# Graph layer pair on one core: the third hop in seven products, with the result transposed back in 128-row blocks

## The chip, the cores and the metric

The kernel runs on one core of one Trainium2 chip. The metric is the time of one execution on the device, in microseconds (us). Lower is better.

## The reference, cut to what matters

The input is `x`, 8 batches of 2048 nodes with 64 features, and `adj`, a 2048 x 2048 matrix. Each row of `adj` has about ten entries that are not zero, and all of one row are equal: `adj[n, m] = r[n]` where two nodes are joined or equal, else 0. Two layers follow each other, each ends in a layer norm over the 64 features.

```python
# layer 0: K = 3, weights of their own for each node, from an embedding of 16 numbers
w = einsum('nd,dkio->nkio', embedding, weight)
As = [I, A, 2*(A @ A) - I]
out = einsum('bnki,nkio->bno', einsum('knm,bmc->bnkc', stack(As), x), w) + einsum('nd,do->no', embedding, bias)
x = layernorm(x + out)
# layer 1: both supports are adj
x_stack = [x0, A x0, 2 A (A x0) - x0, A x0, 2 A (A x0) - x0]
out = concatenate(x_stack, -1) @ weight + bias          # (5*64, 64)
x = layernorm(x + out)
```

So each layer needs `A` and `A A` applied to something. In layer 1 the features can be multiplied by the weights first, and that is what the kernel does: with `u2`, `u1`, `u0` = the normed features times three 64 x 64 matrices, the output is `u0 + A (u1 + A u2)`.

## The kernel before, in words

`kernel()` calls `gnn_kernel`, which runs `pattern` (the fast path, all that is timed here) and, if a flag says that `adj` has not the form told above, `general`.

The matrix is used as a mask of zeros and ones (`s`, exact in the float32r type), and the row's value `r` is multiplied in afterwards. A feature tile (128 nodes by 512 numbers, 8 batches x 64) is split in a high and a low half (`high` on ScalarE, L209; `low` on VectorE, L213), so that each product is two float32r matmuls. There are 16 tiles of 128 nodes. `z[0]`, `z[1]`, `z[2]` hold three such sets of tiles in SBUF.

There are four hops, with layer 0's mixing between the second and the third.

1. *First hop* (`hop_x`, `add_block` L229): `A x`, 512 matmuls, in two halves of eight output tiles. Masks are made by `places` (L198: not equal 0). Alongside, `put_together` writes sums and differences of the four quarters of the mask (L393) to device memory as bfloat16, `sums_of`, from GpSimd's queue, and `seen` (L445) counts the entries.
2. *Second hop* (`seven_products`): `A (A x)` by seven products of quarter matrices rather than eight. A product is eight steps; a step has 8 matmuls (L529) with the feature sum as the stationary operand, and the mask sum (256 KB from `sums_of`, cast by ScalarE at L517) or the mask itself (a 512 KB slab and `places`) as the moving one. The result is therefore transposed, features by nodes, which is what layer 0's mixing needs. `put` adds each product into the quarters of `z[2]` that need it (L550). 448 matmuls.
3. *Layer 0's mixing* (`mix0`, one tile of 128 nodes after another): for each of two halves of the batches and four groups of embedding numbers, 12 matmuls on float32 (L342, two instructions each), and four accumulations on VectorE that weight the result by the embedding (L348). Before the last group, `between()` transposes the normed features of the tile before (`transpose`, L268, copied by ScalarE at L270) and `A x` of the next tile. After the tile, `layernorm` (L306 to L312) and `project` of the tile before (L361, L368, L369) give `u2`, `u1`, `u0` in `z[0]`, `z[1]`, `z[2]`.
4. *Third hop* (`hop_h`): `A u2` for output tiles 0 to 3, 8 to 15 and 4 to 7, each group over 16 steps; a step makes its mask with `places_equal` (L205: equal to the row's value, with a count) and the halves of `z[0][k]`. 512 matmuls (L229). `evict` (L260 on VectorE; L257 and L258 on ScalarE and GpSimd) adds `r` times the sum to `z[1]`.
5. *Fourth hop*: output tiles 0 to 7 by `hop_g`, 16 steps of 16 matmuls, which also keeps the halves of `z[1]` for later; then tiles 8 to 15 one at a time by `hop_tile`, each in two halves of 16 matmuls. Behind it run the last norms (`square_sums`, `rsqrt`) and the stores.

What sets the order: `run(steps)` goes through a list of steps, and every step has parts with a lead (a part with lead 2 is written two steps ahead of the use). After each step two entries of the list `todo` are written. While `in_order` is not empty, `ordered(...)` keeps instructions in the order of the program on their engine; otherwise the tile framework's scheduler may move them. Loads go on SyncE's queue in program order. PSUM is a pool of four tiles of two banks each, handed on in turn (`bank`).

The last tile of layer 0 is projected inside the third hop: `hop_h`'s last step of the first group does it, and only there does `in_order` begin.

Of the kernel before, what the change touches and what calls it, by code (L numbers as in the profile page):

```python
# [8 lines left out]
F32 = mybir.dt.float32  # L9
# [28 lines left out]
def pattern(  # L38
# [20 lines left out]

    nc = tc.nc  # L60
# [13 lines left out]
    rowpool = pool(hops, "frow", 1, side="right")  # L74
    hpool = pool(hops, "fhl", HL, side="right")
# [23 lines left out]
    equal = keep.tile([P, 3 * NT], F32, tag="equal", name="equal")  # L99
# [13 lines left out]
    v = const.tile([P, 3, C], F32, tag="v", name="v")  # L113
# [122 lines left out]
    def run(steps):  # L236

        got = [{} for _ in steps]
        for i in range(-6, len(steps)):
            for ahead in range(6, -1, -1):  # L240
                for lead, part in steps[i + ahead] if 0 <= i + ahead < len(steps) else ():
                    if lead == ahead:
                        part(got[i + ahead])
            for _ in range(2):
                if todo and i >= 0:
                    todo.pop(0)()
# [15 lines left out]
    def transpose(src, tag, pt=None):  # L262
# [7 lines left out]
        nc.scalar.copy(  # L270
            tt.rearrange("p j (h n) -> p h j n", h=2), pt[:, :, : B // 2 * C].rearrange("p h (j n) -> p h j n", n=C)
        )
# [5 lines left out]
    def rsqrt(ss):  # L278
# [6 lines left out]
        nc.vector.scalar_tensor_tensor(va, ss, 1.0 / C, eps.to_broadcast(list(ss.shape)), ALU.mult, ALU.add)  # L285
        sd = col("ln_sd")
        nc.scalar.activation(sd, ss, AF.Sqrt, bias=eps, scale=1.0 / C)  # L287
        r0 = col("ln_r0")
        nc.vector.reciprocal(r0, sd)

        q = col("ln_q")
        nc.vector.scalar_tensor_tensor(q, r0, -0.5, r0, ALU.mult, ALU.mult)
        nc.vector.tensor_tensor(q, q, va, ALU.mult)
        r = col("ln_r")
        nc.vector.scalar_tensor_tensor(r, q, 1.5, r0, ALU.add, ALU.mult)
        return r

    def square_sums(src, to):
        sq = work.tile([P, B, C], F32, tag="ln_sq", name="sq")
        nc.scalar.activation(sq, src, AF.Square)  # L300
        nc.vector.tensor_reduce(to, sq, AX.X, ALU.add)

    def layernorm(src):

        s = work.tile([P, B], F32, tag="ln_s", name="s")
        nc.vector.tensor_reduce(s, src, AX.X, ALU.add)  # L306
        nc.vector.tensor_tensor(s, s, part, ALU.mult)  # L307
        xc = xcpool.tile([P, B, C], F32, tag="ln_xc", name="xc")
        nc.gpsimd.tensor_tensor(xc, src, wide(s), ALU.subtract)  # L309
        ss = work.tile([P, B], F32, tag="ln_ss", name="ss")  # L310
        square_sums(xc, ss)
        nc.gpsimd.tensor_tensor(xc, xc, wide(rsqrt(ss)), ALU.mult)  # L312
        return xc
# [7 lines left out]
    def mix0(t, tt, between):  # L321
# [4 lines left out]
        for g in range(2):  # L326
# [6 lines left out]
            for dg in range(D // DG):  # L333
                if g == 1 and dg == D // DG - 1:
                    between()
# [10 lines left out]
                for d in range(DG):  # L346
                    dd = dg * DG + d
                    nc.vector.scalar_tensor_tensor(  # L348
                        part, pm[:, :, :, d, :].rearrange("p j i c -> p (j i) c"), emb_sb[:, t, dd : dd + 1], part, ALU.mult, ALU.add
                    )  # L350
        return layernorm(acc)

    def project(t, hT, pus=None):


        for g in range(2):
# [9 lines left out]
            bs = slice(4 * g, 4 * g + 4)  # L366
            for s in range(2):
                nc.scalar.copy(bc(s, t)[:, bs, :].rearrange("p (i j) c -> p j i c", j=2), got[:, :, :, 2 - s, :])  # L368
            nc.vector.tensor_tensor(  # L369
                bc(2, t)[:, bs, :].rearrange("p (i j) c -> p j i c", j=2), got[:, :, :, 0, :],  # L370
                bias1.unsqueeze(1).unsqueeze(1).to_broadcast([P, 2, 2, C]), ALU.add,
            )
# [10 lines left out]
    S1, S2, S4, S3 = range(4)  # L383
    couple = []
# [11 lines left out]
    def hop_x(g, kk, j):  # L396
# [37 lines left out]
        def use(got):  # L434
# [8 lines left out]
            seen = work.tile([P, 2, Q], BF16, tag="ln_sq", name="seen")  # L443
            i = g * NT + k
            ordered(nc.scalar.activation(seen, s, AF.Copy, accum_out=nonzero[:, i : i + 1]))  # L445
            if last and g == 1:

                todo.extend(lambda i=i: out(i) for i in range(4, 8))
# [11 lines left out]
    def seven_products(s, to, more):  # L460
# [3 lines left out]
        sums, kept = [], {}  # L464

        def sum_of_y(kk, name):
# [11 lines left out]
            if name == "T2":  # L478
# [4 lines left out]
                return add(y, add(y, quarter(2, 2), quarter(1, 2), ALU.subtract), quarter(1, 1), ALU.add)  # L483
            y = xcpool.tile([P, BC], F32, tag="ln_xc", name="y")
            if name == "T4":
                return add(y, kept[kk // 2][:, kk % 2], quarter(2, 1), ALU.subtract)
# [3 lines left out]
        def step(p, kk):  # L490
# [5 lines left out]
            def y_high(got):  # L496
                hl = hpool.tile([P, 2, BC], F32R, tag="hl", name="hl")
                got["hl"] = [hl[:, 0], hl[:, 1]]
                if name[0] == "B":
                    sum_y(got)  # L500
# [5 lines left out]
            def load_sum(got):  # L506
                if isinstance(which, tuple):
                    return
                raw = got["raw"] = rawp.tile([P, 2, Q], BF16, tag="raw", name="raw")
                load(nc.sync, raw, sums_of[kk, :, :, which, :].rearrange("g m n -> m g n"))  # L510

            def operands(got):
                if isinstance(which, tuple):
                    got["s"] = places(slab(kk + KK * which[1], which[0] * HALF, HALF))
# [7 lines left out]
            def use(got):  # L522
# [10 lines left out]
                if p == 0 and kk == 3:  # L533
                    node_bias(sums[1])
                    todo.extend(lambda h=h: keep_node_bias(sums[1], h) for h in range(2))
                if kk < KK - 1:
                    return
                if p < 6:
                    todo.extend([lambda: None] * 4)
                for i in range(2):  # L540
                    for c in range(2):
                        todo.append(lambda i=i, c=c: put(acc[i][:, c], i, c))
                todo.extend(more.get(p, ()))
# [21 lines left out]
            before = [(5, sum_y)] if name[0] != "B" else []  # L565
# [8 lines left out]
    def times_r(t):  # L574
# [6 lines left out]
    pieces = weights()  # L581
    more = {
        1: [lambda: ordered(next(pieces)) for _ in range(13)],
        5: [lambda: times_r(0), lambda: times_r(1)],
    }
    run([hop_x(g, kk, j) for g in range(2) for kk in range(KK) for j in range(2)] + seven_products(1, to_z2, more))
# [13 lines left out]
    def hop_h(g, first, n, k):  # L600
        def operands(got):
            if g == 0 and k == NT - 1:
                project(mixed[0], transpose(mixed[1].rearrange("p b c -> p (b c)"), "hT"))
                layer0.close()
                in_order.append(True)
            i = g * NT + k
            raw = slab(k, first * P, n * P)
            got["s"], got["hl"] = places_equal(raw, first * P, equal[:, i : i + 1]), halves(z[0][k])

        def use(got):  # L610
            s, hl = got["s"], got["hl"]
            if k == 0:
                accs[:] = banks(n)
            add_block(accs, s, hl, k == 0, k == NT - 1)
            if k == NT - 1:
                for i, a in enumerate(accs):
                    evict(z[1][first + i], first + i, a, i % 2)

        return [(2, operands), (0, use)]

    third = [hop_h(g, first, n, k) for g, (first, n) in enumerate(((0, 4), (8, 8), (4, 4))) for k in range(NT)]

    mixed = None
    tt = operands(0)
    for t in range(NT):
        done = {}

        def between():
            if mixed is not None:
                done["hT"] = transpose(mixed[1].rearrange("p b c -> p (b c)"), "hT")  # L630
# [5 lines left out]
        new = t, mix0(t, tt, between)  # L636
        tt = done.get("tt")
        if mixed is not None:
            project(mixed[0], done["hT"])
        mixed = new  # L640
# [7 lines left out]
    def check():  # L648
# [3 lines left out]
        tc.keep_in_program_order(nc.vector.tensor_tensor(bad, count("n_nz", nonzero), count("n_eq", equal), ALU.not_equal))  # L652
        tc.keep_in_program_order(nc.vector.tensor_add(bad, bad, count("n_0", zeros)))
        ones = work.tile([P, 1], F32, tag="ones", name="ones")
        tc.keep_in_program_order(nc.vector.memset(ones, 1.0))
        pf = bank("pf")
# [11 lines left out]
    EARLY = 8  # L668
    late = []
    ks = [0, 1, 2, 3, 8, 9, 10, 11, 12, 13, 14, 15, 4, 5, 6, 7]  # L670
    hls = {}
    sums = keep.tile([P, 8, B], F32, tag="sums", name="sums")
    late_values = {}

# [384 lines left out]
```

## Time and profile before

| | us |
|---|---|
| median of 3 runs (837.89 to 840.62) | 839.54 |
| the profiled execution's own time | 839.63 |
| its span, first to last instruction | 837.6 |
| mean granted TensorE clock | 0.994 |
| first hop, first to last matmul step | 5.9 to 122.5 |
| second hop | 122.5 to 225.3 |
| layer 0's mixing, up to the third hop's first matmul | 225.3 to 592.0 |
| third hop and the fourth's steps | 592.0 to 769.9 |
| the fourth hop's tiles | 769.9 to 827.8 |
| last norm and store | 827.8 to 837.6 |

The span is what the profiler recorded between the first and the last instruction; the time of the execution has 2.0 us more around it. All engines share one time axis. PE is TensorE's matmuls, PEld its weight loads, DVE VectorE, ACT ScalarE, POOL GpSimd, SP SyncE. In a group of instructions the columns are: line, engine, operation, output <- inputs, sizes, count, then busy time and mean nanoseconds of one, then the engine's idle time before them and what ended it. Matmuls overlap each other, so a mean duration of 390 ns goes with a step of less than 230 ns from start to start. A line can be that of a helper.

### The profile page before, as it was taken

The numbers are of one execution on the slowest core, as the hardware profiler recorded it, in microseconds if no ns is written. First come the engines' busy times: TensorE is split into PE (matmuls) and PEld (weight loads), VectorE is DVE, ScalarE is ACT, GpSimd is POOL, SyncE is SP. The second block draws the span as 40 slices with busy tenths as digits, with TensorE's granted clock in tenths as the row PEclk, the third lists the DMA queues.
The fourth block names the chain that finished last, engine by engine and source line by source line (L and its number), as shares of the span: only waits on it lengthen the run. The fifth ranks groups of instructions, "written<-read, shape, count | busy, mean of one in ns | idle before, by whom it ended". The sixth has DMA issues, their size and how long they took to land.

```text
span 837.6 us, 14392 instructions
## 1 busy us (share of the span) xinstructions
PE 823.5 (98%) x5614; PEld 732.0 (87%) x5614; DVE 607.0 (72%) x1256; ACT 224.6 (27%) x427; POOL 128.8 (15%) x130
## 2 busy tenths in 40 slices
PE   9999999999999999999999999989999999999995
PEld 6888888888888999999999999989888878888884
DVE  6868657757878888888788888897867567534662
ACT  5436445772002111111111111101331132401210
POOL 0100000002731111111111111020101020102133
PEclk9999999999999999999999999999999999999998
DMA  9976775558200000000000000120256227544462
GB/s 332 394 273 221 248 258 174 154 163 289 88 14 14 11 6 13 14 14 13 14 14 13 14 14 14 42 86 2 76 182 190 94 74 240 173 142 126 132 183 92
DMA packets 57180, 96.55 MB, mean 115 GB/s; under 512 B 3984, under 2 KB 28816, under 8 KB 56976
## 3 DMA queue, kind: packets, MB, share of 16 engines
q1 hardware_dynamic: 52208, 82.69, 30.6%
q0 software_dynamic: 2304, 8.39, 3.0%
q10 hardware_dynamic: 2592, 4.47, 1.5%
q8 instruction: 47, 0.77, 0.4%
q14 instruction: 29, 0.24, 0.1%
HBM read 82.94 MB, written 12.58 MB: 114 GB/s over the span
## 4 chain that ended last, share of the span: by engine, by line
PE 93%; DVE 4%; issue 1%; DMA 0%; ACT 0%; POOL 0%; SPq 0%; DVEq 0%; POOLq 0%
PE pm L342 36%; PE acc L229 35%; PE accT L529 12%; PE a L229 7%; DVE acc L348 3%; PE pu L361 2%; PE pt L268 1%; PE first L133 1%; DVE s L205 0%; DMA raw<-in_adj 0%; POOL got L318 0%; DVE s L306 0%; ACT L287 0%; PE accT L144 0%; POOL xc L309 0%
## 5 line engine op out<-in xcount | busy, mean ns | idle before, releaser
L229 PE MATMUL acc<-hl,s 128*128 128x512 f32 x1280 | 292.7, 390 | 0.3 <-DVE acc L348 0.3
L229 PEld LDWEIGHTS acc<-hl,s 128*128 128x128 f32 x1280 | 239.4, 188 | 52.9 <-issue 1.2
L348 DVE SCALAR_TENSOR_TENSOR acc<-pm,pack_sb,acc 128x256 f32<-128x256 f32 x512 | 246.3, 483 | 43.5 <-PE pm L342 21.1
L342 PE MATMUL pm<-w,xt 64*128 64x256 f32 x1024 | 161.1, 379 | 3.1 <-DVE acc L348 2.8
L342 PE MATMUL pm<-w,z 64*128 64x256 f32 x1024 | 160.4, 378 | 0.0
L342 PE MATMUL pm<-w,t 64*128 64x256 f32 x1024 | 160.1, 377 | 0.2 <-ACT t L270 0.2
L342 PEld LDWEIGHTS pm<-w,xt 64*128 64x128 f32 x1024 | 108.1, 188 | 5.6 <-issue 1.8
L342 PEld LDWEIGHTS pm<-w,t 64*128 64x128 f32 x1024 | 110.7, 188 | 2.0 <-ACT t L270 0.6
L342 PEld LDWEIGHTS pm<-w,z 64*128 64x128 f32 x1024 | 110.8, 188 | 1.4
L198 DVE TENSOR_SCALAR s<-raw 128x1024 fp32r<-128x1024 f32 x87 | 68.1, 783 | 57.8 <-PE acc L229 48.8
L529 PE MATMUL accT<-s,hl 128*128 128x512 f32 x448 | 102.0, 389 | 0.0
L529 PEld LDWEIGHTS accT<-s,hl 128*128 128x128 f32 x448 | 84.0, 188 | 17.5
L209 ACT CAST hl<-z 128x512 fp32r<-128x512 f32 (+1 forms) x120 | 67.0, 578 | 119.1 <-PE acc L229 108.5
L213 DVE TENSOR_TENSOR hl<-z,hl 128x512 fp32r<-128x512 f32 (+1 forms) x120 | 81.5, 681 | 13.6 <-ACT hl L209 10.7
L205 DVE SCALAR_TENSOR_TENSOR s<-raw,rrow 128x512 fp32r<-128x512 f32 (+1 forms) x48 | 45.8, 956 | 26.7 <-PE acc L229 25.3
L270 ACT COPY hT<-pt 128x512 f32<-128x512 f32 x16 | 9.4, 586 | 204.4 <-PE pt L268 204.4
L309 POOL TENSOR_TENSOR xc<-acc,s 128x512 f32<-128x512 f32 x16 | 17.1, 1068 | 282.4 <-DVE s L307 282.4
L229 PE MATMUL a<-hl,s 128*128 128x512 f32 x256 | 58.5, 390 | 0.0
L229 PEld LDWEIGHTS a<-hl,s 128*128 128x128 f32 x256 | 48.0, 188 | 10.0
L258 POOL TENSOR_TENSOR z<-z,got 128x512 f32<-128x512 f32 x12 | 18.8, 1592 | 155.2 <-ACT got L257 155.1
L328 POOL TENSOR_TENSOR acc<-z,ebias 128x256 f32<-128x256 f32 x32 | 27.0, 866 | 87.1 <-ACT hl L209 85.6
L517 ACT CAST s<-raw 128x1024 fp32r<-128x1024 bf16 x32 | 33.6, 1050 | 10.6 <-ACT hl L209 10.6
(87 smaller groups left out, 477.0 us busy)
## 6 DMA issues: line engine op xcount, KB each, us to landing
raw<-in_adj SPq DMA_DIRECT2D x103, 512.0 KB, 4.5
raw<-in_adj SPq DMA_DIRECT2D x34, 256.0 KB, 3.0
sums_of<-z POOLq DMA_DIRECT2D x16, 512.0 KB, 4.9
raw<-sums_of SPq DMA_DIRECT2D x32, 256.0 KB, 2.8
xt<-in_xT SPq DMA_DIRECT2D x16, 256.0 KB, 2.7
out<-got ACTq DMA_DIRECT2D x16, 256.0 KB, 2.0
z<-in_x SPq DMA_DIRECT2D x15, 256.0 KB, 9.3
w<-in_w SPq DMA_DIRECT2D x3, 512.0 KB, 5.8
```

Of the source, the lines that this page charges most:

```text
L198: ordered(nc.vector.tensor_scalar(s, raw, 0.0, None, ALU.not_equal))
L205: ordered(nc.vector.scalar_tensor_tensor(s, raw, 0.0, r, ALU.add, ALU.is_equal, accum_out=count))
L209: ordered(nc.scalar.copy(to[0], src))
L213: ordered(nc.vector.tensor_tensor(to[1], src, to[0], ALU.subtract))
L229: nc.tensor.matmul(accs[i], lhsT=s[:, i * P : (i + 1) * P], rhs=hl[h], start=(first and h == 0), stop=(last and h == 1),)
L258: ordered(nc.gpsimd.tensor_tensor(to, to, got, ALU.add))
L309: nc.gpsimd.tensor_tensor(xc, src, wide(s), ALU.subtract)
L328: nc.gpsimd.tensor_tensor(part.rearrange("p (j i) c -> p j i c", j=2), bc(0, t)[:, 4 * g : 4 * g + 4, :].rearrange("p (i j) c -> p j i c", ...
L342: nc.tensor.matmul(pm[:, j, i], lhsT=tt[k][q, 2 * g + i, :], rhs=w[k][q, ds, :], start=(k == 0), stop=(k == 2),)
L348: nc.vector.scalar_tensor_tensor(part, pm[:, :, :, d, :].rearrange("p j i c -> p (j i) c"), emb_sb[:, t, dd : dd + 1], part, ALU.mult, ALU.add
L517: ordered(nc.scalar.copy(s, got["raw"]))
L529: nc.tensor.matmul(acc[i][:, c], lhsT=hl[h][:, i * P : (i + 1) * P], rhs=S[:, c * 512 : (c + 1) * 512], start=(kk == 0 and h == 0), stop=( ...
```

## The change

The third hop takes the form of the second: seven products, now over `u2` = `z[0]`. Its result comes out transposed. It is gathered in four new tiles `zT` (with the same `put` as before), turned back with 64 transposes of 128 x 128 into the PSUM banks that the products leave free (`back`), and added to `z[1]` with the row's value (`add_back`). Each quarter is turned back when it is complete: three quarters as entries of `todo` inside products 5 to 7, the fourth in steps 1 and 3 of the fourth hop.

The operands of its first four steps are made by `early(i)` in layer 0's tiles 12 to 15, written between groups 6 and 7 of 8 of a tile. In tile 15 the projection of tile 14 stands after the sixth group; tile 15's own projection is written in steps 5 and 7 of the third hop, into the banks of the second product. The norm and the projection of every tile are now in program order.

Around it: `quarters` keeps the right-hand quarters of the mask, as bfloat16, in device memory (written from `seen` on ScalarE's queue in the first hop), and both sevens-of-products read them instead of slabs where the mask itself is wanted, all but product 1. The sums T4 are formed in place during product 4. The fourth hop is split 6 and 10, not 8 and 8, and its masks are now made by equality with a count; the check of the form and its flag move to the last two tiles.

```diff
-    rowpool = pool(hops, "frow", 1, side="right")
-    hpool = pool(hops, "fhl", HL, side="right")
+    rowpool = pool(ctx, "frow", 1, side="right")
+    hpool = pool(ctx, "fhl", HL, side="right")
...
     def layernorm(src):
-        nc.vector.tensor_reduce(s, src, AX.X, ALU.add)
-        nc.vector.tensor_tensor(s, s, part, ALU.mult)
+        ordered(nc.vector.tensor_reduce(s, src, AX.X, ALU.add))
+        ordered(nc.vector.tensor_tensor(s, s, part, ALU.mult))
         xc = xcpool.tile([P, B, C], F32, tag="ln_xc", name="xc")
-        nc.gpsimd.tensor_tensor(xc, src, wide(s), ALU.subtract)
-        ss = work.tile([P, B], F32, tag="ln_ss", name="ss")
-        square_sums(xc, ss)
-        nc.gpsimd.tensor_tensor(xc, xc, wide(rsqrt(ss)), ALU.mult)
-        return xc
+        ordered(nc.gpsimd.tensor_tensor(xc, src, wide(s), ALU.subtract))
+        yield xc.rearrange("p b c -> p (b c)")
+        sq = squares(xc)
+        yield
+        ss = work.tile([P, B], F32, tag="ln_ss", name="ss")
+        ordered(nc.vector.tensor_reduce(ss, sq, AX.X, ALU.add))
+        root = rsqrt_parts(ss)
+        next(root)
+        yield
+        ordered(nc.gpsimd.tensor_tensor(xc, xc, wide(next(root)), ALU.mult))
+        yield
...
             for dg in range(D // DG):
-                if g == 1 and dg == D // DG - 1:
-                    between()
+                for work_here in at.get((g, dg), ()):
+                    work_here()
...
+    quarters = scratch.tile([KK, P, 2, 2, Q], BF16, tag="quarters", name="quarters")
...
-            seen = work.tile([P, 2, Q], BF16, tag="ln_sq", name="seen")
+            seen = xcpool.tile([P, 2, Q], BF16, tag="ln_xc", name="seen")
             i = g * NT + k
             ordered(nc.scalar.activation(seen, s, AF.Copy, accum_out=nonzero[:, i : i + 1]))
+            if j == 1:
+                ordered(nc.scalar.dma_start(out=quarters[kk, :, :, g, :], in_=seen))
...
-    def seven_products(s, to, more):
+    def seven_products(s, to, sums, more, wait=4):
...
             def load_sum(got):
-                if isinstance(which, tuple):
+                if which == (0, 0):
                     return
                 raw = got["raw"] = rawp.tile([P, 2, Q], BF16, tag="raw", name="raw")
-                load(nc.sync, raw, sums_of[kk, :, :, which, :].rearrange("g m n -> m g n"))
+                if isinstance(which, tuple):
+                    load(nc.sync, raw, quarters[kk, :, which[0]])
+                else:
+                    load(nc.sync, raw, sums_of[kk, :, :, which, :].rearrange("g m n -> m g n"))
...
+                if p == 3:
+                    sum_of_y(kk, "T4")
+                for f in more.get((p, kk), ()):
+                    f()
...
-    def hop_h(g, first, n, k):
...
+    def last_transposed():
+        last_h["T"] = transpose(h, "hT", sums3[1][0])
+
+    def last_projected():
+        project(NT - 1, last_h["T"], (sums3[1][1], sums3[1][0]))
+        layer0.close()
...
+    def to_zT(a, b, i, c):
+        return zT[a, c][:, :, (2 * b + i) * P : (2 * b + i + 1) * P]
+
+    def back(ts, pairs, b):
+        to = [pairs[n // 4][:, n // 2 % 2, n % 2 * BC : (n % 2 + 1) * BC] for n in range(len(ts))]
+        for t, a in zip(ts, to):
+            for i in range(2):
+                block = slice((2 * b + i) * P, (2 * b + i + 1) * P)
+                nc.tensor.transpose(a[:, i * P : (i + 1) * P], zT[t // 8, t // 4 % 2][:, t % 4, block], ident)
+        return to
+
+    def add_back(t, a, b):
+        to = z[1][t][:, b * BC : (b + 1) * BC]
+        ordered(nc.vector.scalar_tensor_tensor(to, a, rcol[:, t : t + 1], to, ALU.mult, ALU.add))
...
+        work_here = [nothing, nothing, lambda: got.extend(back(ts, sums3[which], b)), nothing]
+        return work_here + [lambda n=n: two(n) for n in range(0, 8, 2)]
+
+    third = seven_products(0, to_zT, sums3, {
+        (0, 5): [last_transposed],
+        (0, 7): [last_projected],
+        3: quarter_back(1, 1, 1), 4: quarter_back(0, 1, 0), 5: quarter_back(0, 0, 1),
+    }, wait=2)
+
+    def early(i):
+        in_order.append(True)
+        got = third_got[i] = {}
+        for lead, part in sorted(third[i], key=lambda part: -part[0]):
+            if lead > 0:
+                part(got)
+        third[i] = [part for part in third[i] if part[0] == 0]
+        in_order.pop()
...
+        at = {(1, 3): [between]}
+        if t == NT - 1:
+            in_order.append(True)
+            at = {(1, 0): [between], (1, 1): [lambda: project(t - 1, done["hT"])]}
+        if t >= NT - 4:
+            at[1, 2] = [lambda: early(t - NT + 4)]
+        norm = mix0(t, tt, at)
...
-    EARLY = 8
+    G = 6
...
-            got["s"] = places(slab(k, 0, HALF))
+            got["s"] = places_equal(slab(k, 0, G * P), 0, equal[:, k : k + 1])
...
-                accs[:] = banks(8)
-            add_block(accs, s, hl, k == ks[0], k == ks[-1])
+                pairs = [*sums3[1], sums3[0][0]]
+                accs[:] = [p[:, i] for p in pairs for i in range(2)]
+            add_block(accs[:4], s, hl, k == 0, end)
+            waiting.append((s[:, 4 * P :], hl, k == 0, end))
+            if k > 0:
+                while waiting:
+                    add_block(accs[4:], *waiting.pop(0))
+            if k in (1, 3):
+                ts = range(8, 12) if k == 1 else range(12, NT)
+                for t, a in zip(ts, back(ts, [sums3[0][1]], 0)):
+                    add_back(t, a, 0)
...
-    run(third + [hop_g(k) for k in ks] + [hop_tile(t, c) for t in range(8, NT) for c in range(2)])
+    run(third + [hop_g(k) for k in range(NT)] + [hop_tile(t, c) for t in range(G, NT) for c in range(2)], third_got)
```

## The prediction

> **What bounds the kernel now.** I read the head of the page first, then the chain of waits, then a table of windows by stage, then the timeline of the two places where the chain leaves TensorE.
>
> ```profile
> span 837.6 us, 14392 instructions
> PE 823.5 (98%) x5614; PEld 732.0 (87%) x5614; DVE 607.0 (72%) x1256; ACT 224.6 (27%) x427; POOL 128.8 (15%) x130
> PE 93%; DVE 4%; issue 1%; DMA 0%; ACT 0%; POOL 0%; SPq 0%; DVEq 0%; POOLq 0%
> ```
>
> TensorE is busy nearly throughout and is 93% of the chain that ended last. So only two things move the end: fewer TensorE microseconds, or fewer of its gaps. The table of windows (sum of the window, then PE, PEld, DVE, ACT, POOL busy, granted clock, DMA share, GB/s) says where gaps are: a normal tile of layer 0, then the stretch before its end, then the third and fourth hops.
>
> ```profile
> 20.00:110.00 90.00, 90.00 (x399) 74.32 (x398) 68.47 (x108) 43.28 (x78) 6.93 (x13) 1.00 0.83 287
> 474.54:497.11 22.57, 22.57 (x227) 22.52 (x225) 18.32 (x43) 3.30 (x9) 3.51 (x4) 1.00 0.05 13
> 542.00:569.76 27.76, 25.47 (x230) 24.31 (x228) 22.25 (x51) 3.63 (x10) 4.66 (x4) 0.94 0.27 88
> 620.00:765.00 145.00, 144.96 (x638) 119.08 (x637) 84.41 (x142) 33.65 (x58) 13.34 (x8) 1.00 0.49 153
> ```
>
> A normal tile takes 22.57 us with no TensorE gap. The tile from 542.0 takes 27.76, with 2.3 us of gap and a granted clock of 0.94. The chain in order of time (start, length, what) names the cause:
>
> ```profile
> 519.68 18.13 PE pm L342 x168
> 537.81 0.49 PE pt L268 x16
> ...
> 540.50 3.19 DMA raw<-in_adj
> ...
> 546.14 3.26 DVE s L205 x6
> ...
> 563.92 4.52 PE pm L342 x24
> 568.44 1.32 PE pu L361 x16
> 569.76 18.13 PE pm L342 x168
> ```
>
> VectorE made the third hop's first four operands (L205) inside this tile, and waited 1.2 us for the first one's load. In a normal tile it has only 0.92 us to spare (its one wait for TensorE per tile in the timeline). Its accumulations (L348) came late, TensorE waited 0.75 and 1.7 us for PSUM, and after that the same 24 matmuls took 4.52 us instead of the usual 2.65. The projection before this tile ended at 542.06 and the next at 569.76, 27.7 us where 22.6 is normal.
>
> The groups give the prices.
>
> ```profile
> L229 PE MATMUL acc<-hl,s 128*128 128x512 f32 x1280 | 292.7, 390 | 0.3 <-DVE acc L348 0.3
> L529 PE MATMUL accT<-s,hl 128*128 128x512 f32 x448 | 102.0, 389 | 0.0
> L268 PE MATMUL pt<-ident,z 64*128 64x64 f32 x128 | 7.1, 224 | 0.1
> L517 ACT CAST s<-raw 128x1024 fp32r<-128x1024 bf16 x32 | 33.6, 1050 | 10.6 <-ACT hl L209 10.6
> ```
>
> A mean duration is not a price, because matmuls overlap; the step from start to start is. The second hop (L529) runs from 122.55 to 225.30 with 1.05 us of node bias in it: 101.7 us for 448, 0.2270 each. From the third hop's first matmul (592.02) to the fourth's tile part (769.92) there are 768 matmuls in 177.9 us, less 0.5 of wait at the start and 1.9 of transposes and projection: 0.2285 each.
>
> **The change, part by part.**
>
> *Removed matmuls.* The third hop has 16x16x2 = 512 matmuls (L229) and gets 7x8x8 = 448. Minus 64 at 0.2285: **-14.6 us**. The 448 that stay take the second hop's form, which has 0.2270: **-0.7**.
>
> *Added transposes.* The result comes out transposed, so 16 tiles x 4 blocks = 64 transposes of 128x128 float32 are added, on TensorE, in four batches of 16 (the last in two of 8). The trace has no such form. Nearest is L268, whose 16 transposes (64 rows, 64 columns, two side by side in the array) take 0.49 us: 61 ns for a pair. Mean durations of the float32 forms rise evenly with columns: 223 ns at 64, 324 at 192, 378 at 256, about 0.8 ns per column. So 128 columns add about 53 ns to a pair's 61: 0.115 us each, **+7.4 us** for 64. From below: 61 ns (the number of columns hidden by weight loads), 3.9 us. From above, the Trainium skill, "TensorE: Matmul & The Clock Gate", section "Part 4: PE-mode transpose", speaks against the change: a 128x128 transpose took about 275 ns in a kernel and 390 alone, and does not count as activity for the clock. At 275 the 64 cost 17.6 us and eat the whole saving of 14.6. I take 0.115: the rule's figure is of the order of this trace's L268 *duration* (223 ns), and the trace shows that durations overlap here, 16 of them in 0.49 us. A batch of 16 is then 1.8 us, and the granted clock stayed 1.00 in all windows with L268 in them but the stalled one.
>
> *The end of layer 0.* The changed kernel makes each of the first four steps' operands in one of the last four tiles, between the sixth and seventh group of accumulations. That is one load (512 KB, on SP's queue behind the tile's xt load, a tile ahead of its use), one cast on ACT (0.40) and two operations on VectorE (0.42 for the low half, 0.70 for the mask; start to start 0.34 and 0.61). So each tile bears 0.95 us more against 0.92 us to spare. The changed order also takes the sum for the norm ahead of the projection's bias addition (L369, 0.41), which starts the chain POOL, ACT, VectorE about 0.4 us sooner. TensorE's last group waits only for the sixth group, ahead of the insertion. Cost taken: 0; bounds 0 and 1.0 for each of three tiles, 3.0. What goes: 27.70 - 22.57, less the 0.2 us that the projection before ended early, **-4.9**. The projection of tile 14 moves inside tile 15 (same work), and the first hop matmul no longer waits for VectorE's last accumulations (the 0.5 us from 592.5 to 593.0), since its PSUM banks are older: **-0.5**.
>
> *What is late next: step 4 of the third hop.* Steps 0 to 3 last 4 x 1.82 = 7.3 us. VectorE ends its last accumulation 2.1 us after TensorE's last mix, then runs the norm: sum 0.68 and 0.17, POOL 1.05, ACT 0.63, sum 0.69, root and Newton 1.2, the low halves of steps 4 and 5 (0.34 each) and step 4's mask: ready at about 8.1. A wait of 0.85. From then on VectorE needs about 1.65 us a step (two T2 sums, low half, mask) against 1.82. Second wait: the last projection writes the banks of the second product, so step 8 waits until VectorE has read them. In the trace the first L369 after the late projection (617.85) ended at 619.9, 0.8 us after TensorE was through. ACT then has four copies (1.3) and the first product's four evictions (0.58 each) beside 1.45 us a step: 0.2 more. Together **+1.8**, bounds 0 and 4.
>
> *The batches inside the hop.* Each comes three steps after its product's end, 7.3 us; VectorE's evictions before it are at most eight additions at 0.61 and two low halves, 5.6. The eight add-backs after it (0.45 each) end about 3 us before the bank is wanted. Queued behind them are low halves made three steps ahead. Cost 0, upper bound 1 us a batch, 4. For the fourth hop's start, the last product's first two evictions are 1.4 us, covered by 16 matmuls (3.6 us) on other banks.
>
> *Fourth hop.* 6 column tiles by steps and 10 by tiles instead of 8 and 8: 512 matmuls as before. Steps run at 0.2285, tiles at 0.225 (769.92 to 827.8, 256): 64 move, **-0.2**. Its masks become equality tests with a count (L205's form, 1.2 for 1024 columns against 0.7); VectorE then has 1.7 of a 2.7 us step and about 5 of a 7.3 us tile. Cost 0. The flag's load (0.47 to 0.54 per queue in the trace) falls into the last tile's second half, before its norm. Cost 0, upper bound 0.6.
>
> *First and second hop.* 16 writes of 256 KB from ACT's queue are added (4.2 MB; issue 0.34 each). ACT has 43 of 90 us in this stage, so the issue is hidden. DMA is at 0.83 and 287 GB/s; the first half of the stage would ask for 2.3 MB in 7.3 us, 316 GB/s, and the page shows 394 in one slice. Cost 0, upper bound 4.2 MB at 287 GB/s, 14.6. In products 6 and 7 of the second hop a mask on VectorE (0.7) and a 512 KB load become an ACT copy (1.05) and 256 KB: ACT 1.45 of 1.82, as in the products before. T4's sums move to product 4, where VectorE has about 1.4 of 1.82. Cost 0.
>
> **Sum:** -14.6 - 0.7 + 7.4 - 4.9 - 0.5 + 1.8 - 0.2 = **-11.7 us**. The profiled execution's own time is 839.63 (span 837.6 and 2.0 around it), 0.1 above the median of the runs: 827.9, or **827.8** beside the median.
>
> **Rivals.**
> 1. *VectorE becomes the bound around the border of the layers.* For it: 0.92 us to spare against 0.95 added. Against: the insertion stands after what TensorE waits for. With 3.0 in the tiles and 4 in the hop's start, not 1.8, and 1 at a batch: -11.7 + 6.2, 834.1. Faster still.
> 2. *The transposes cost what the skill says*, 275 ns: +10.2, 838.1, no change. Break-even is at 0.30 us each. Against: the 0.49 us for 16.
> 3. *The new writes starve the first hop*: slower. The place is the first 58 us, DMA share 0.9 in two slices. If the writes are not overlapped, +14.6: 842.5. It decides once more than 11.7 us shows as TensorE waiting for masks. Against: VectorE waits 48.8 us for TensorE to free masks and 3.3 for loads there.
> 4. *Step operands made early change nothing* (VectorE late anyway): -11.7 + 5.4, 833.3. It shares its range with rival 1.
>
> **How the numbers follow.** Forecast 0.72, rivals 1 and 4 together 0.15, rival 2 0.07, rival 3 0.06. The forecast's own range is 822.5 (61 ns a transpose, no new waits) to 831. Rivals 1 and 4 reach 834.5; rivals 2 and 3 stay outside. A measurement of this kernel can tell about 0.3% (2.5 us) from no change: faster 0.87, same 0.07, slower 0.06.
>
> **What would show it.** After: 64 transposes with 16 of them in 1.6 to 2.0 us; tiles 12 to 15 at 22.6 us and clock 1.00; no mask for the third hop in one block in a tile; a wait of about 1 us before step 4 and before step 8; first and second hop unchanged at 116.6 and 102.8 us. Wrong if a batch takes over 4 us, if TensorE waits before a batch, or if the first hop has gaps.

## The result, and the profile after

The changed kernel takes 828.5 us (828.30 to 828.83, 4 runs) where the kernel before took 839.1 (837.89 to 840.62, 4 runs of that session): a ratio of 0.9873, 95% interval 0.9856 to 0.9891. The profiled execution took 828.66, its span is 826.8. Against the profiled execution of before (839.63) that is -11.0 us.

The head of the page, and the chain by engine:

```profile
span 826.8 us, 14470 instructions
PE 812.6 (98%) x5614; PEld 725.2 (88%) x5614; DVE 594.7 (72%) x1303; ACT 275.3 (33%) x496; POOL 111.9 (14%) x121
PE 92%; issue 3%; DVE 3%; POOL 1%; ACT 1%; DVEq 0%; POOLq 0%; ACTq 0%
```

TensorE is still the bound. It has as many instructions as before, because 64 hop matmuls became 64 transposes, but 10.9 us less busy time: a count says nothing of the price. The windows (sum, PE, PEld, DVE, ACT, POOL busy, granted clock, DMA share, GB/s) are, in order: the first hop, a normal tile of layer 0, the tile in which the kernel before stalled, the first 19 us of the third hop, the rest of that hop, and the fourth hop's steps.

```profile
20.00:110.00 90.00, 90.00 (x399) 74.33 (x398) 68.96 (x109) 43.39 (x78) 6.93 (x13) 1.00 0.93 327
474.49:497.06 22.57, 22.57 (x226) 22.53 (x225) 18.42 (x43) 3.30 (x9) 3.50 (x4) 1.00 0.11 37
542.19:564.75 22.56, 22.56 (x226) 22.52 (x225) 19.26 (x45) 3.58 (x10) 3.50 (x4) 1.00 0.32 105
587.10:606.15 19.05, 17.14 (x89) 13.29 (x89) 14.09 (x34) 6.91 (x16) 2.14 (x2) 1.00 0.34 98
606.15:698.87 92.72, 92.72 (x433) 77.44 (x434) 55.59 (x132) 67.40 (x103) 0.00 (x0) 1.00 0.47 145
698.87:744.20 45.33, 45.33 (x209) 37.69 (x209) 31.22 (x61) 5.11 (x10) 0.00 (x0) 1.00 0.57 163
```

The tile from 542.19 takes 22.56 us with no gap and the clock at 1.00; it was 27.70 from projection to projection, with the clock at 0.94. The only gap is in the first 19 us of the third hop: 19.05 - 17.14 = 1.91 us. The first hop keeps TensorE busy throughout at a DMA share of 0.93 (0.83 before). The chain in order of time (start, length, what):

```profile
579.31 7.78 PE pm L361 x72
587.12 0.49 DVE acc L367
...
594.32 1.46 DVE s L200
595.91 3.94 PE accT L558 x16
599.85 0.39 PE accT L274 x8
600.24 3.85 PE accT L558 x16
604.09 0.88 PE accT L380 x8
604.99 0.66 ACT z L387 x2
605.67 0.43 DVE z L388
606.15 51.09 PE accT L558 x224
657.24 1.75 PE accT L662 x16
658.99 14.55 PE accT L558 x64
673.54 1.75 PE accT L662 x16
675.29 14.53 PE accT L558 x64
```

A batch of 16 back-transposes (L662) stands between two stretches of hop matmuls and takes 1.75 us from start to start, 0.109 each. The same instructions in the groups:

```profile
L662 PE MATMUL accT<-ident,zT 128*128 128x128 f32 x64 | 7.8, 273 | 0.0
```

One *lasts* 273 ns. That is near the 275 ns of the Trainium skill, "TensorE: Matmul & The Clock Gate", section "Part 4: PE-mode transpose" (measured there on bfloat16 in one kernel); but 64 of them take 7.0 us (three batches of 1.75 and two of 0.87), not 17.5, because they overlap.

### The profile page after: what moved, and what is told of

The parts are those of the page before. It is cut to its first block, busy times and chain, and to the rows that moved or that the text cites. A ratio compares the mean times of both kernels' runs of the same rounds, so it can differ in the third digit from the quotient of the medians.

```text
span 826.8 us, 14470 instructions
## 1 busy us (share of the span) xinstructions
PE 812.6 (98%) x5614; PEld 725.2 (88%) x5614; DVE 594.7 (72%) x1303; ACT 275.3 (33%) x496; POOL 111.9 (14%) x121
## 4 chain that ended last, share of the span: by engine, by line
PE 92%; issue 3%; DVE 3%; POOL 1%; ACT 1%; DVEq 0%; POOLq 0%; ACTq 0%
PE pm L361 36%; PE accT L558 24%; PE acc L231 14%; PE a L231 8%; PE accT L231 5%; PE pu L380 2%; DVE acc L367 2%; POOL z L609 1%; PE pt L274 1%; PE accT L662 1%; PE first L135 1%; POOL xc L322 0%; POOL got L337 0%; ACT sq L310 0%; DVE s L200 0%
## 5 line engine op out<-in xcount | busy, mean ns | idle before, releaser
L558 PE MATMUL accT<-s,hl 128*128 128x512 f32 x896 | 205.6, 390 | 1.9 <-DVE s L200 1.4
L558 PEld LDWEIGHTS accT<-s,hl 128*128 128x128 f32 x896 | 167.6, 188 | 37.7 <-issue 1.8
L231 PE MATMUL acc<-hl,s 128*128 128x512 f32 x512 | 117.1, 390 | 0.0
L546 ACT CAST s<-raw 128x1024 fp32r<-128x1024 bf16 x96 | 101.0, 1052 | 40.2 <-ACT hl L211 32.2
L231 PEld LDWEIGHTS acc<-hl,s 128*128 128x128 f32 x512 | 95.8, 188 | 21.1 <-DVE hl L215 0.7
L211 ACT CAST hl<-z 128x256 fp32r<-128x256 f32 (+1 forms) x96 | 47.1, 510 | 67.6 <-PE acc L231 36.4
L215 DVE TENSOR_TENSOR hl<-z,hl 128x512 fp32r<-128x512 f32 (+1 forms) x96 | 52.5, 552 | 21.2 <-ACT hl L211 18.4
L200 DVE TENSOR_SCALAR s<-raw 128x1024 fp32r<-128x1024 f32 x47 | 33.2, 706 | 16.5 <-PE acc L231 10.9
L231 PE MATMUL accT<-hl,s 128*128 128x512 f32 x192 | 44.2, 390 | 0.0
L231 PEld LDWEIGHTS accT<-hl,s 128*128 128x128 f32 x192 | 35.9, 188 | 7.4
```

The source lines that it names most:

```text
L200: ordered(nc.vector.tensor_scalar(s, raw, 0.0, None, ALU.not_equal))
L211: ordered(nc.scalar.copy(to[0], src))
L215: ordered(nc.vector.tensor_tensor(to[1], src, to[0], ALU.subtract))
L231: nc.tensor.matmul(accs[i], lhsT=s[:, i * P : (i + 1) * P], rhs=hl[h], start=(first and h == 0), stop=(last and h == 1),)
L546: ordered(nc.scalar.copy(s, got["raw"]))
L558: nc.tensor.matmul(acc[i][:, c], lhsT=hl[h][:, i * P : (i + 1) * P], rhs=S[:, c * 512 : (c + 1) * 512], start=(kk == 0 and h == 0), stop=( ...
```

## The experiments

Differences are of the medians, against the changed kernel's run just below (the base). Only "transposes twice", "quarter writes twice" and "both" ran on its chip in its session; for the others the ratio to the kernel before, or a stretch of the trace, is given beside the difference.

**The changed kernel again**, as the base.

> The changed kernel itself, so that the variants can be set beside it on the same chip. Expected: 828.5 us, ratio to before 0.987; third hop's 448 matmuls at about 0.228 us, waits of 1.36 and 0.56 us before its steps 4 and 8.

Measured: 828.29 us, ratio 0.9868 (0.9853 to 0.9883). The third hop begins at 587.20 and its waits end as in the first profile.

**Transposes twice** (rival 2).

```diff
-                nc.tensor.transpose(a[:, i * P : (i + 1) * P], zT[...][:, t % 4, block], ident)
+                for _ in range(2):
+                    nc.tensor.transpose(a[:, i * P : (i + 1) * P], zT[...][:, t % 4, block], ident)
```

> Every back-transpose of the third hop is issued twice in a row into the same place; the result is the same. Theory (a 128 x 128 float32 transpose in a stream costs 0.109 us of TensorE, although it lasts 0.273): 64 more cost 64 x 0.109 = +7.0 us over the changed kernel, 835.5, and a batch of 32 takes 3.5 us. Rival (the 0.275 us of the rule is the price, and the first 64 were partly hidden by something else): +17.6 us, 846. Rival (the batches lie in time that TensorE has free): 0. The granted clock stays at 1.00 in the windows with batches by the first theory; by the rule that transposes don't count as activity it would dip when a batch lasts twice as long.

Measured: 835.17 us, +6.9 over the base. The chain, and the windows of one doubled batch and of the matmuls behind it:

```profile
657.09 3.50 PE accT L663 x32
660.58 14.55 PE accT L558 x64
675.14 3.49 PE accT L663 x32
```

```profile
657.09:660.58 3.49, 3.49 (x33) 3.49 (x32) 1.71 (x5) 1.35 (x2) 0.00 (x0) 1.00 0.46 150
660.58:668.00 7.42, 7.42 (x35) 6.09 (x34) 3.94 (x10) 4.10 (x7) 0.00 (x0) 1.00 0.20 71
```

A batch of 32 takes twice a batch of 16, and the hop matmuls around it are untouched. The price is 0.109 us, whole, with nothing hidden. The second statement of that section of the skill, that transposes do not count as activity for the clock, does not show here: the granted clock is 1.00 in 3.5 us of nothing but transposes and in the 7.4 us behind them. No run has a longer stretch of transposes.

**Quarter writes twice** (rival 3).

```diff
-                ordered(nc.scalar.dma_start(out=quarters[kk, :, :, g, :], in_=seen))
+                for to in (quarters, again):
+                    ordered(nc.scalar.dma_start(out=to[kk, :, :, g, :], in_=seen))
```

> Each of the 16 writes of the mask's right-hand quarters (256 KB) in the first hop is issued twice, the second time to a place that nobody reads: 4.2 MB more in the first hop. Theory (the DMA share of 0.93 there is still off the path, since ScalarE and VectorE have slack and the loads are issued ahead): 0, at most +1 us, first hop 116.6 us without a TensorE gap. Rival (at 0.93 the engines are all but full; 4.2 MB at 327 GB/s are 12.8 us): TensorE waits for masks in the first half of the hop, up to +12.8 us, 841; in between if only the first, denser half counts, about +6.

Measured: 828.62 us, +0.3 over the base, ratio 0.9875 (0.986 to 0.9891). In the first hop:

```profile
20.00:110.00 90.00, 90.00 (x399) 74.32 (x398) 68.64 (x108) 44.72 (x81) 6.91 (x13) 1.00 1.01 362
```

The DMA share, as the profile counts it, is at 1.01, and 362 GB/s are moved, and TensorE still has no gap in 90 us. Rival 3 is not near its point of decision even with twice the writes.

**No quarters at all.** The writes are taken out, and products 6 and 7 of both hops make their masks from slabs of the matrix.

```diff
-            if j == 1:
-                ordered(nc.scalar.dma_start(out=quarters[kk, :, :, g, :], in_=seen))
...
-                if which == (0, 0):
-                    got["s"] = places(slab(kk, 0, HALF))
+                if isinstance(which, tuple):
+                    got["s"] = places(slab(kk + KK * which[1], which[0] * HALF, HALF))
```

> The mask's right-hand quarters are not written to device memory; products 6 and 7 of the second and third hop make their masks from slabs of the matrix (512 KB) on VectorE, as products of the second hop did before the change. Theory: 0, within 0.5 us of 828.3 (VectorE has the 0.7 us of a mask to spare in a step of 1.82, also with two of the eight add-backs of 0.45 in it; the 16 writes were hidden). Rival (in the third hop VectorE has the evictions, the add-backs and the masks in products 6 and 7 together, up to 0.7 + 0.34 + 0.9 a step, over 1.82): TensorE waits in products 6 and 7, +1 to +3 us.

Measured: 827.87 us, ratio 0.9872 (0.9856 to 0.9889) where the base has 0.9868: no difference. In the third hop from 606.15 on VectorE is busy 65.53 of 92.72 us instead of 55.59, ScalarE 51.35 instead of 67.40, and TensorE 92.72 in both. So this part of the change moves work from VectorE to ScalarE where neither is the bound.

**No early operands** (rival 4).

```diff
-        if t >= NT - 4:
-            at[1, 2] = [lambda: early(t - NT + 4)]
```

> The third hop keeps its seven products, but the operands of its first four steps are no longer made inside layer 0's last four tiles; they are written after tile 15 like those of every later step. Theory (the early operands are what lets TensorE go from the last mixing into the hop without a gap): a TensorE gap of about 4 us at the hop's first step (VectorE ends its accumulations 2.1 us after TensorE, then has the low halves of steps 0 to 3, 0.34 each, and the first masks, 0.7 each), and the norm and the waits behind it later by about as much: +4 to +7 us, 832.5 to 835.5. Rival (VectorE is late at the border anyway, and the early operands only move its work): within 1 us of 828.3.

Measured: 834.58 us, ratio 0.9950 (0.9933 to 0.9967); +6.3 over the base's 828.29, +6.9 by the ratios. From the last mixing's end to the fourth hop's first matmul the trace has 118.24 us for the base's 111.75, +6.5. TensorE's timeline at the border, and two windows of its first matmuls there:

```profile
586.86 0.62 PE L361 MATMUL pm<-w,z 64*128 64x256 f32 x4
592.75 13.93 PE L558 MATMUL accT<-s,hl 128*128 128x512 f32 x48 [5.27 <-DVE s L200]
```

```profile
592.75:600.00 7.25, 7.25 (x20) 5.79 (x21) 7.01 (x18) 1.52 (x5) 1.09 (x1) 0.59 0.74 225
600.00:606.68 6.68, 6.68 (x32) 5.26 (x32) 5.78 (x14) 0.51 (x2) 0.00 (x0) 1.00 0.60 187
```

The wait is 5.27 us, and then the clock averages 0.59 over 7.25 us: the first 48 matmuls take 13.93 us, where 48 take 11.10 in the kernel without waits below. So the gap costs 5.27 + 2.8; the wait before step 4 (1.36) is gone in return, which leaves 6.7, near what was measured. The time lies in the range expected, but by other terms: the gap was to be about 4, the clock had been left out, and the later wait went where it was to grow. Rival 4 is out.

**The two new waits.** The last norm is written two steps later, the last projection one step earlier; each alone, and both.

```diff
-        (0, 7): [last_projected],
+        (0, 6): [last_projected],
...
+            todo.extend([nothing] * 4)
             todo.extend(lambda: next(norm) for _ in range(3))
```

> Only the last tile's norm is written two steps later, its projection stays at step 7. Theory (the wait before step 4 is the masks and low halves queued behind the norm on VectorE): the wait of 1.36 us before step 4 goes. The one before step 8 comes from the last bias addition reading the banks that step 8 writes; the norm ends nearer to the projection now, but the projection's place is the same, so it stays at about 0.56 us: -1.4 us, 826.9. Rival (the norm is now so late that the projection at step 7 waits): no gain, a gap of 1 us or more before the projection.

> Only the last projection is written one step earlier (step 6, not 7), the norm stays where it was. Theory (the 0.56 us before step 8 are VectorE's reading of the projection's banks): it goes, the 1.36 before step 4 stays, -0.6 us, 827.7. Rival (with the norm in its old place the wait before step 8 is of the norm's end, not of the projection's place): 0.

> The parts of the last tile's norm are written two steps of the third hop later, and its projection one step earlier (step 6, not 7). Theory (the wait of 1.36 us before step 4 is the low halves and the mask queued on VectorE behind the norm, the 0.56 before step 8 is VectorE's late reading of the projection's banks): both waits go, -1.9 us, 826.6. Rival (VectorE simply has too much to do in the first eight steps, so that the wait comes at another step): no change, within 0.5 us of 828.5, with one wait of about as much at steps 5 to 8. Second rival (the later norm makes the projection late for the second product, whose banks it uses): slower by 1 to 3 us, with a TensorE gap at step 6 to 8.

| | us | ratio to before | hop's first matmul to step 8 |
|---|---|---|---|
| base | 828.29 | 0.9868 (0.9853 to 0.9883) | 19.04 |
| projection earlier | 827.39 | 0.9870 (0.9853 to 0.9886) | 18.47 |
| norm later | 826.52 | 0.9857 (0.9840 to 0.9873) | 17.40 |
| both | 826.19 | 0.9843 (0.9829 to 0.9856) | 16.85 |

The last column is from each chain (where the 232 matmuls of one piece begin a step early, one step of 1.82 is added). The stretch gets shorter by 0.57, 1.64 and 2.19 us: each wait answers to its own cause, and the two add up. The base and "both" ran side by side: -2.1, where -1.9 was expected. The two single ones ran in other sessions and their intervals overlap the base's, so for them the stretch is the evidence, not the time. The chain of "both" does not leave TensorE in the hop:

```profile
587.20 11.10 PE accT L558 x48
598.30 0.39 PE accT L274 x8
598.69 2.04 PE accT L558 x8
600.73 1.50 PE accT L380 x16
602.23 52.86 PE accT L558 x232
```

**Half the columns**: is the transposed form worth its transposes?

```diff
-                        for c in range(2):
+                        w = 512 if s else 256
+                        for c in range(0, 1024, w):
                             nc.tensor.matmul(
-                                acc[i][:, c], lhsT=..., rhs=S[:, c * 512 : (c + 1) * 512],
+                                acc[i][:, c // 512, c % 512 : c % 512 + w], lhsT=..., rhs=S[:, c : c + w],
```

> Each of the third hop's 448 matmuls on 512 columns is written as two on 256, with the same stationary operand loaded for each: 896 in all. This is the shape that an untransposed third hop would have (256 numbers of the features as the moving operand), which needs no transposes back. Theory (a matmul can't follow the last one faster than its weight load, whose mean is 0.129 us by the page: 725.2 us for 5614): 896 at 0.129 or more, 116 us for 102, +14 us, 842; then the transposed form with its 7.0 us of transposes is the cheaper one. Rival (time goes by columns alone): 0, 828.3, and the transposes could be saved.

Measured: 833.89 us, ratio 0.9944 (0.9928 to 0.9961), +5.6 (+6.4 by the ratios; +5.2 in the trace, 116.97 us from the hop's first matmul to the fourth's). The theory of +14 falls. Its price was 725.2 us of busy time over 5614 loads; busy time counts overlapped loads once and gaps not at all, so it is not a step from start to start. The chain has that step:

```profile
606.54 54.02 PE accT L559 x448
```

That is 0.1206 each; 512 columns cost 0.228, so a half is 0.0066 us dearer than half of one. For 896 of them that is 5.9 us, less than the 7.0 of the transposes; those before the wait at step 4 cost nothing in this run, since VectorE ends that wait.

**Without transposes.** So the hop was written with its operands' roles exchanged.

```diff
-                for i in range(2):
+                for n in range(8 if s == 0 else 0):
+                    to_n = acc[n // 4][:, n // 2 % 2, n % 2 * BC : (n % 2 + 1) * BC]
+                    for h in range(2):
+                        nc.tensor.matmul(to_n, lhsT=S[:, n * P : (n + 1) * P], rhs=hl[h], ...)
+                for i in range(2 if s else 0):
...
-        return zT[a, c][:, :, (2 * b + i) * P : (2 * b + i + 1) * P]
+        return zT[a, c][:, 2 * b + i, :].rearrange("p (t n) -> p t n", n=P)
...
-                nc.tensor.transpose(a[:, i * P : (i + 1) * P], zT[t // 8, t // 4 % 2][:, t % 4, block], ident)
-        return to
+        return [zT[t // 8, t // 2 % 2][:, 2 * b + t // 4 % 2, t % 2 * BC : (t % 2 + 1) * BC] for t in ts]
```

> The third hop's seven products with the operands' roles exchanged: the mask sum is the stationary operand (128 nodes), the 256 numbers of the feature sum the moving one. The result is not transposed; it is gathered in the same four tiles and added to z[1] from there, and the 64 transposes back are gone. 896 matmuls on 256 columns for 448 on 512. Theory: in half_columns 448 matmuls on 256 columns took 54.02 us, 0.1206 each, where 224 on 512 took 51.08 in after_again; so 896 cost 5.9 us more, and the 64 transposes at 0.109 cost 7.0 less: -1.1 us, 827.2. Rival (a weight load of a mask sum, or two matmuls in a row into one bank half, is slower than of the feature sums in half_columns): slower than 828.3. Rival (the two halves of a feature sum follow each other on one stationary operand, and the second load is cheaper): faster than 826.

Measured: 826.81 us, ratio 0.9860 (0.9844 to 0.9877): 1.5 below the base, 0.7 by the ratios, and the intervals overlap; a single further run of the same kernel took 826.36. So the traces are the evidence. The third hop from its first matmul to the fourth's takes 111.76 us (587.72 to 699.48), as long as in the changed kernel (111.77, with three batches in it), and the fourth hop's steps take 43.55 instead of 45.33, because the last two half batches are gone: -1.8.

**Both together.**

> The third hop without transposes (as in upright) together with both moves of both_waits (the last norm two steps later, the last projection a step earlier). Theory (the two gains are on different parts of the hop and add up): 826.81 - 2.1 = 824.7 us, no TensorE wait in the hop. Rival (without transposes VectorE's work comes closer together, and a wait appears in products 6 and 7 or at the fourth hop's start): about 826.

Measured: 824.81 us (824.56 to 825.25, 5 runs), ratio 0.9833 (0.9820 to 0.9847). The sum of the two gains was 824.7. This is the fastest kernel here, 13.7 us below the kernel before on the same chip (838.55). Its chain from the last mixing on:

```profile
578.98 7.77 PE pm L361 x72
586.75 11.70 PE accT L558 x96
598.45 0.39 PE accT L274 x8
598.84 2.10 PE accT L558 x16
600.94 1.50 PE accT L380 x16
602.45 94.26 PE accT L558 x784
696.71 43.55 PE accT L231 x192
740.25 65.29 PE a L231 x288
```

No other engine is in it for 226 us. In the window of most of this hop the weight loads are nearly as busy as TensorE (92.31 of 92.72 us), which suggests, without showing it, that loads now set the step:

```profile
606.15:698.87 92.72, 92.72 (x766) 92.31 (x765) 56.34 (x131) 65.55 (x100) 0.00 (x0) 1.00 0.47 148
```

## Why the prediction was right, point by point

Predicted -11.7 us, 827.8; measured -11.0 in the profiled executions. The hop's start moved from 592.02 to 587.10 (-4.9), and from there to the last matmul it takes 6.1 us less, where the prediction's terms for that stretch make -6.8.

- *The end of layer 0, -4.9.* Right: 27.70 became 22.56 for the tile, the last mixing ended at 587.09. The insertion costs TensorE nothing, as taken: VectorE is busy 19.26 us in such a tile, 18.42 in a normal one, and still waits 0.37 us for TensorE, so rival 1 had nothing to work with there. One reading of the old stall was off: the 0.75 us is a wait of the weight load; TensorE's own wait there was 0.38, at 553.4, ten microseconds before the one of 1.68. And VectorE was late in part because of GpSimd (last section), which the prediction did not see. Neither enters the sum. The kernel without early operands shows the part to be worth 6.3 to 6.9 in the new hop, more than the 5.4 of rival 4.
- *The hop's first matmul without a wait, -0.5.* Right: the last mixing ends at 587.09 and the hop begins at 587.10.
- *Added transposes, +7.4.* Right, 7.0. The bounds (3.9 and 17.6) were far apart, and the row of the 64 x 64 form was the better guide than the skill's figure, since it had a step from start to start in it. Doubling them confirms the price.
- *Removed matmuls, -14.6, and the better rate of those that stay, -0.7.* The second is the term that failed. The pieces of the chain and the first 32 (7.45 us) sum to 102.7 us for 448, 0.2293 each, and not 101.7 at 0.2270. Runs of 64 in the middle do have the rate taken (14.53 to 14.55 us, 0.227); 0.7 of the missing 1.0 us is in the first 64, in three short pieces cut by waits and by the 64-row forms. Even without waits the 8 matmuls between those forms take 2.04 us, where 1.82 is normal. A rate read from a long undisturbed hop was carried to one that begins in pieces. ("64-row forms" are the small transposes and the projection, L274 and L380, whose stationary operand fills 64 of the 128 rows.)
- *New waits, +1.8.* The sum was right (1.91), but by luck, since its parts missed in opposite directions: 1.36 before step 4, not 0.85; 0.56 before step 8, not 0.8 and another 0.2 from ScalarE. What made the first one longer was the mask of step 4, taken at 0.7 and measured at 1.53, beside GpSimd (see the last section); a later norm removes the queue and this meeting together, so the runs do not price them apart. The 0.8 was a misreading: in the trace before, that addition ended at 619.92 and the projection at 619.42, 0.5 apart. And ScalarE is in the second wait after all. VectorE's addition stood until ScalarE's first two copies out of the same PSUM banks (0.66 us) were done, although it does not use what they write; why it stood is not shown:

```profile
604.99 1.30 ACT L387 COPY z<-accT 128x256 f32<-128x256 f32 x4 [1.55 <-PE accT L380]
605.67 0.42 DVE L388 TENSOR_TENSOR z<-accT,pack_sb 128x256 f32<-128x256 f32 x1 [2.44 <-ACT z L387]
```

- *The batches inside the hop, 0.* Right: TensorE is busy 92.72 of 92.72 us from 606.15 on.
- *Fourth hop, -0.2.* 192 matmuls in 43.6 us without the transposes, and 288 in 65.29: 0.227 in both forms. For 512 (192, and 320 at 0.2267) that is 116.1, where 256 at 0.2285 and 57.9 made 116.4 before.
- *First and second hop, 0.* Right to 0.2 us: the first hop takes 116.8 us (116.4 in the changed kernel's second profile, 116.6 before), the second still 102.8 (122.80 to 225.55). ScalarE waits longer for the loads of `x` (15.3 us in all, 6.3 before), but TensorE has no wait in this hop.

Against -11.7 the rate is 1.0 worse, the transposes 0.4 better, the waits 0.1 worse: +0.7, which is the difference.

## What to carry to other kernels

Price an instruction by the step from start to start of a row of its kind, never by its duration and never by busy time over count: the first mistake would have made this change look useless (17.5 us of transposes for 7.0), and the second made the form without transposes look 14 us dear when it was 5.6. When a bound engine changes from one stage to the next, prepare the first few steps' operands inside the stage before, in slots that the other engines have free, and then look at which part of the old stage's end is queued ahead of the new stage's work: moving two such entries by a step or two gave 2.1 us. And a detour that a layout forces (here transposes back) should be priced against the slower form that needs no detour.

## What the runs showed of the hardware

VectorE's mask operation takes 0.7 us (mean 706 ns of 47), but the one before step 4 took 1.53. GpSimd's second pass of the norm ran just then. From the timelines of VectorE and of GpSimd in the changed kernel:

```profile
594.23 1.53 DVE L200 TENSOR_SCALAR s<-raw 128x1024 fp32r<-128x1024 f32 x1
596.81 0.68 DVE L200 TENSOR_SCALAR s<-raw 128x1024 fp32r<-128x1024 f32 x1
```

```profile
594.12 1.09 POOL L331 TENSOR_TENSOR xc<-xc,ln_r 128x512 f32<-128x512 f32 x1 [2.85 <-DVE ln_r L302]
```

GpSimd ends at 595.21, the mask 0.55 us later, about a whole mask operation: it seems to have stood until GpSimd was through. In each of the ten profiles with the norm in its old place the mask that meets this pass takes 1.53 or 1.54 us. The Trainium skill has a rule for it ("SBUF — State Buffer", section "SBUF: two separate sides"): the two engines have one pair of SBUF ports in common, and a GpSimd operation and a VectorE operation that needs the pair (one with two inputs in SBUF, or one in a two-port mode) exclude each other, the first holding it for its whole instruction. That the mask, with its one input, runs in such a mode is not shown here. With the norm later GpSimd's pass meets another operation: in the kernel with both moves an addition with two inputs, at 595.94, takes 1.15 us instead of 0.43, beside GpSimd's 595.71 to 596.80. There it costs TensorE nothing: the mask behind it still ends at 598.03, before its step begins at 598.69.

The kernel before had the same in the tile that stalled:

```profile
546.28 1.43 POOL L309 TENSOR_TENSOR xc<-acc,s 128x512 f32<-128x512 f32 x1 [19.70 <-DVE s L307]
546.77 1.49 DVE L205 SCALAR_TENSOR_TENSOR s<-raw,rrow 128x512 fp32r<-128x512 f32 x1
548.19 1.20 DVE L205 SCALAR_TENSOR_TENSOR s<-raw,rrow 128x512 fp32r<-128x512 f32 x1
```

Two of the four masks took 1.49 and 1.20 us, where the others took 0.69; the first of the two ended 0.55 us after GpSimd did. So 1.3 us of VectorE's lateness there lay beside GpSimd's work, and the new place, between the sixth and seventh group, has none of it (0.68 to 0.69 us for the masks of tiles 12 to 15).

The clock: a TensorE wait of 1.36 us left it at 1.00; one of 5.27 us was followed by 7.25 us at 0.59 on average, so that a gap of 5.3 cost 8.1. But in the kernel before, a wait of only 1.68 us, behind 16 small transposes, was followed by a slow stretch (from the timeline, then its window):

```profile
563.92 0.70 PE L342 MATMUL pm<-w,xt 64*128 64x256 f32 x4 [1.68 <-DVE acc L348]
```

```profile
563.92:568.44 4.52, 4.52 (x27) 4.36 (x29) 1.89 (x4) 0.00 (x0) 0.00 (x0) 0.62 0.00 0
```

The clock averages 0.62, and the 24 matmuls take 1.9 us more than their usual 2.65. These runs do not show how short a wait is safe.
